# A Perceiver cross-attention's context values, computed 128 rows at a time across batches

## The chip, the cores and the metric

The kernel runs on one core of a Trainium2 chip. The metric is the device time of one execution in microseconds (us); the time before is the median of three runs. All arithmetic is in 32-bit floats. A batch norm, an exponential, a copy and the like run on VectorE (DVE), ScalarE (ACT) or GpSimd (POOL); matrix products and transposes run on TensorE (PE); SyncE's queue (SP) issues the DMAs. PEld is TensorE's loading of stationary operands, which overlaps its matmuls.

## The reference, cut to what matters

The model has two layers, each a gated cross-attention and a gated feed-forward block, on `x` (16 batches, 256 tokens, 256 features) with contexts of 77 tokens:

```python
x = x + tanh(g_xattn[0]) * L0_xattn(ctx, layernorm(x), ...)   # stage 0: Perceiver attention
x = x + tanh(g_ffn[0])   * L0_ffn(layernorm(x), ...)          # stage 1: 8 experts, the top 2 of a token
x = x + tanh(g_xattn[1]) * L1_xattn(layernorm(x), ctx, ...)   # stage 2: masked cross-attention
x = x + tanh(g_ffn[1])   * L1_ffn(layernorm(x), ...)          # stage 3: gated linear attention
```

The change lies in stage 0, whose attention is

```python
def L0_xattn(image_embeds, latents, ln1_g, ln1_b, ln2_g, ln2_b, Wq, Wkv, Wo):
    x = layer_norm(image_embeds, ln1_g, ln1_b)      # 16 x 77 x 256, the contexts
    l = layer_norm(latents, ln2_g, ln2_b)           # 16 x 256 x 256, the latents
    q = l @ Wq                                      # 256 x 1024: 16 heads of 64
    kv = concatenate([x, l], axis=1) @ Wkv          # 333 tokens x 2048
    k, v = split(kv, 2, axis=-1)
    w = softmax(q * 64 ** -0.25 @ (k * 64 ** -0.25).T)   # per batch and head, 256 x 333
    return (w @ v) @ Wo
```

Keys and values of a batch thus run over 333 tokens: 256 latents and 77 contexts.

## The kernel before

**Stages.** The four stages run one after the other. Stage 0 takes the first half of the time, then come the experts, the second attention and the gated linear attention. Routing work of stage 1 (logits, choice, scatter of rows) is done inside stage 0, batch by batch, between the attention's steps. Weights come in by DMA: those of stages 0 and 1, and `wq2`, `wk2`, `wv2`, `wo2` of the second attention (256 KB each, loaded at L133), at the start of the kernel; those of stage 3 later, into a pool that reuses stage 0's memory once that stage is over (`w3`, L778).

**A batch in stage 0.** Batch b's 77 context rows are one DMA (`load_c`, L110 to 112). Contexts and latents are normed on their own (`norm_c`, L552; `normed_all`, L565). `turn` (L571) transposes both on PE into one PSUM pair, and DVE writes them with scale and shift into `kvT`, 333 columns: latents first, then contexts. `all_values` (L586) computes the values of the 333 tokens as three chunks of `KC` = 111 rows: per chunk 2 halves of 512 columns times 2 steps over the features, so 4 matmuls; ACT copies one half of the result out of PSUM, DVE the other. `heads` (L603) computes queries and keys of two heads at a time: 2 + 2 matmuls into one PSUM pair, then ACT scales the queries and DVE copies the keys, both into the tile `qk`.

**A unit.** The attention runs over 64 units (b, g), g being a group of four heads, that is two head pairs n = 0 and 1, each with three chunks of keys c. `scores` (L617) has six steps u = 3n + c of two matmuls each; these fill three PSUM pairs, two steps to a pair, and ACT takes the exponential of each pair. POOL adds the chunks for the softmax's denominators (`sums`, L632). `values` (L641) multiplies by the values of the batch and divides; `project` (L672) applies the output weights once per batch.

**The order.** It is written out by hand in the loop over units (L711 to 751), and the engines' instructions keep it (`Pinned`, L50, so nearly all instructions of stage 0 carry line 50 in the profile; those of stage 3 carry line 1548). On PE a unit is: its scores; then the values of the unit before; in group 1 the turn of the next batch and the projection of the batch before; in group 2 the next batch's `all_values`; then `heads` of the next unit, first n = 0, then n = 1, and straight after them that unit's scores:

```python
now = scores(b, g)
...
now = sums(*now)
if behind is not None:
    values(*behind)
if g == 1 and b + 1 < B:
    turn(b + 1)
if g == 1 and b > 0:
    project(b - 1)
...
if g == 2 and b + 1 < B:
    all_values(b + 1, *route.weighted(b - 2))
if ahead is not None:
    heads(*ahead, 0)
    heads(*ahead, 1)
```

At the start two short bursts of matmuls (`warm`) are issued before the first batch. SP's DMAs go out in one order too: among them the 16 clears of 640 KB in the first two batches, the experts' inputs (`fetch`, L1074, `xin`) and the experts' row stores (L1099), and masks and contexts of the second attention (L1018 to 1024).

Of the kernel before, what the change touches and what calls it, by code (L numbers as in the profile page):

```python
# [73 lines left out]
def layers(ctx: ExitStack, tc: tile.TileContext, t, out, check):  # L74
# [30 lines left out]
    w12 = s12.enter_context(tc.tile_pool(name="s12w", bufs=1, side="right"))  # L105
    ws1 = s1.enter_context(tc.tile_pool(name="s1w", bufs=1, side="right"))
    if fast:
        ctxs = s0.enter_context(tc.tile_pool(name="f0c", bufs=3))

    def load_c(b):  # L110
        cs[b] = ctxs.tile([S2, D], F32, tag="c", name="c")
        nc.sync.dma_start(out=cs[b], in_=t["ctx"][b])

    load_x(0)
    if fast:
# [14 lines left out]
    ew1 = load_w("ew1", D, 2048, ws1)  # L130
    prio = const("prio", [P, 8])
    nc.sync.dma_start(out=prio, in_=t["prio"])
    wq2, wk2, wv2, wo2 = (load_w(n, D, D, w12) for n in ("wq2", "wk2", "wv2", "wo2"))  # L133
    if fast:
        both, own, pmask = (w12.tile(shape, F32, tag=n, name=n) for n, shape in (
            ("both", [P, 2, D]), ("own", [P, 2, 32]), ("pmask", [P, 2])))
# [233 lines left out]
    class Route:  # L370
# [162 lines left out]
    def stage0_fast():  # L533
        with ExitStack() as sx:
# [5 lines left out]
            def pair(name):  # L540
                return pairs.tile([P, 2, 512], F32, tag="ps", name=name)
# [3 lines left out]

            esum, rsum = check["esum"], check["rsum0"]

            xn, cn, kvT, v, oT = {}, {}, {}, {}, {}

            y, mvs, tallies = {}, {}, []  # L550

            def norm_c(b):  # L552
                mvs[b, "c"] = moments(cs[b].unsqueeze(1), S2, 1)

            def norm_x(b):
                mvs[b, "x"] = moments(xs[b])
# [7 lines left out]

            def normed_all(b):  # L565
                xn[b] = w1.tile([P, 2, D], F32, tag="xn", name="xn")
                cn[b] = w1.tile([S2, 1, D], F32, tag="cn", name="cn")
                normed(xn[b], y.pop(b), *mvs.pop((b, "y")))
                normed(cn[b], cs[b].unsqueeze(1), *mvs.pop((b, "c")), S2, 1)

            def turn(b):  # L571
                kvT[b] = w2.tile([P, 2, NK], F32, tag="kvT", name="kvT")
                both = pair("tr")
                for k in range(2):
                    ps = both[:, k, :]
                    for i in range(2):
                        pe.transpose(ps[:, i * P:(i + 1) * P], xn[b][:, i, k * P:(k + 1) * P], ident)
                    pe.transpose(ps[:, S:NK], cn[b][:, 0, k * P:(k + 1) * P], ident[:S2, :S2])
                for k in range(2):
                    ps = both[:, k, :]  # L580
                    dve.tensor_scalar(kvT[b][:, k, :S], ps[:, :S], vec[:, V_LN2G + k:V_LN2G + k + 1],
                                            vec[:, V_LN2B + k:V_LN2B + k + 1], ALU.mult, ALU.add)
                    dve.tensor_scalar(kvT[b][:, k, S:], ps[:, S:NK], vec[:, V_LN1G + k:V_LN1G + k + 1],
                                            vec[:, V_LN1B + k:V_LN1B + k + 1], ALU.mult, ALU.add)

            def all_values(b, *between):  # L586
                v[b] = w2.tile([KC, 3, 1024], F32, tag="v", name="v")
                for c in range(3):
                    both = pair("v")
                    for h in range(2):  # L590
                        ps = both[:, h, :]
                        for k in range(2):
                            pe.matmul(ps[:KC, :], kvT[b][:, k, c * KC:(c + 1) * KC],
                                             wkv0[:, k, 1024 + h * 512:1024 + (h + 1) * 512],
                                             start=k == 0, stop=k == 1)
                    act.copy(v[b][:, c, :512], both[:KC, 0, :])
                    dve.tensor_copy(v[b][:, c, 512:], both[:KC, 1, :])
                    for x in between[c:c + 1]:
                        x()

            qk = {}

# [14 lines left out]
            def scores(b, g):  # L617

                x_qk = qk.pop((b, g))
                e = w2.tile([KC, 6, 2, S], F32, tag="e", name="e")  # L620
                for u in range(0, 6, 2):
                    sc = pair("sc").rearrange("p j (x s) -> p j x s", x=2)
                    for x in range(2):
                        n, c = divmod(u + x, 3)
                        for j in range(2):
                            r = slice(64 * j, 64 * j + 64)
                            pe.matmul(sc[:KC, j, x, :], x_qk[r, n, S + c * KC:S + (c + 1) * KC],
                                             x_qk[r, n, :S], start=True, stop=True)
                    act.activation(e[:, u:u + 2], sc[:KC].rearrange("p j x s -> p x j s"), AF.Exp)
                return b, g, e  # L630

            def sums(b, g, e):  # L632
                es = w2.tile([KC, 2, 2 * S], F32, tag="es", name="es")
                by_chunk = e.rearrange("p (n c) j s -> p n c (j s)", n=2)
                pool.tensor_tensor(es, by_chunk[:, :, 0], by_chunk[:, :, 1], ALU.add)
                pool.tensor_tensor(es, es, by_chunk[:, :, 2], ALU.add)
                for n in range(2):
                    pool.tensor_tensor(esum[:KC], esum[:KC], es[:, n, :], ALU.add)
                return b, g, e, es

            def values(b, g, e, es, last=False):  # L641

                if g == 0:
                    oT[b] = w1.tile([P, 8, S], F32, tag="oT", name="oT")
                both = pair("o")
                den, ps = both[:, 0, :], both[:, 1, :]
                heads = [(h, slice(32 * h, 32 * h + 32)) for h in range(4)]

                for c in range(3 if last else 1):
                    for h, r in heads:  # L650
                        n, j = divmod(h, 2)
                        x = e[:, 3 * n + c, j, :] if last else es[:, n, j * S:(j + 1) * S]
                        pe.matmul(den[r, :S], ones[:KC, :32], x, start=c == 0, stop=not last or c == 2)
                for i in range(2):
                    for c in range(3):
                        for h, r in heads:
                            n, j = divmod(h, 2)
                            lo = (4 * g + h) * 64 + 32 * i
                            pe.matmul(ps[r, i * S:(i + 1) * S], v[b][:, c, lo:lo + 32], e[:, 3 * n + c, j, :],
                                      start=c == 0, stop=c == 2)  # L660
                rd = w2.tile([P, S], F32, tag="rd", name="rd")
                dve.reciprocal(rd, den[:, :S])
                dve.tensor_tensor(oT[b][:, 2 * g:2 * g + 2, :], ps.rearrange("p (i s) -> p i s", i=2),
                                  bc(rd, [P, 2, S], 1), ALU.mult)
                tallies.append((rd, rsum[:, 4 * b + g:4 * b + g + 1]))
# [110 lines left out]


    w3 = ctx.enter_context(tc.tile_pool(name="s3w", bufs=1, reuse_waits="tile"))  # L778

    def c3(name, shape):  # L780
        return w3.tile(list(shape), F32, tag=name, name=name)
# [1314 lines left out]
```

## Time and profile before

| quantity | value |
|---|---|
| median of three runs | 1918.44 us (1918.27 to 1920.98) |
| profiled execution | 1920.95 us |
| span of that execution's trace | 1919.2 us |
| mean granted TensorE clock | 0.995 of full speed |
| PE busy | 1889.1 us, 98% |
| DVE, ACT, POOL busy | 1097.6, 869.8, 992.1 us (57%, 45%, 52%) |
| matmul records | 14028 |
| DMA moved | 75.17 MB, mean 39 GB/s |

The profile is one execution. Its span reaches from the first to the last instruction; the execution's time has 1.75 us around that. A group's row gives busy time and the mean time of one instruction; matmuls are pipelined and overlap in their records, so a matmul's mean is longer than its share of the path. A 32-bit matmul leaves two records. In a row's shapes the stationary operand comes first (`128*111` is 128 partitions by 111 columns), then the moving one. "Idle before" names what the engine waited for. The clock is the one that the throttle granted to TensorE, 1.00 being full speed.

### The profile page before, as it was taken

To read this page: it belongs to the slowest core of one execution; us is meant where nothing else is said; L and a number is where in the kernel's file an instruction comes from. 1 tells how busy PE (TensorE), PEld (TensorE's weight loads), DVE (VectorE), ACT (ScalarE), POOL (GpSimd) and SP (SyncE) were. 2 spreads that over 40 slices of the span, in tenths; PEclk is the share of its full clock that TensorE was granted. 3 is DMA by queue.
4 is the path that set the end of the run, shared out by engine and by line. 5 is a ranking of instruction groups with operands and counts; after the bars stand their busy time and mean duration, and the time that the engine had idled before them with its cause. 6 is when DMAs were issued, how large, how long until landed. Compare 5 with 4: busy or idle time off the path is not lost.

```text
span 1919.2 us, 34996 instructions
## 1 busy us (share of the span) xinstructions
PE 1889.1 (98%) x14028; PEld 1314.7 (69%) x14028; DVE 1097.6 (57%) x2667; ACT 869.8 (45%) x1788; POOL 992.1 (52%) x895
## 2 busy tenths in 40 slices
PE   8999999999999999999999899999999999999997
PEld 5666666666666666666787766667777777777775
DVE  3334555455554555545464388876666666666664
ACT  3333435343353433434343478744444445454442
POOL 4644756557565575655734756314444444444433
PEclk9999999999999999999999999999999999999999
DMA  9300000000000000000068923000000000000000
GB/s 341 138 1 3 14 11 14 7 11 14 11 14 7 11 14 9 12 7 9 12 218 253 225 43 49 15 1 6 7 6 7 6 12 6 7 6 7 12 7 14
DMA packets 54108, 75.17 MB, mean 39 GB/s; under 512 B 10112, under 2 KB 43760, under 8 KB 53424
## 3 DMA queue, kind: packets, MB, share of 16 engines
q1 hardware_dynamic: 41648, 56.05, 8.7%
q0 software_dynamic: 12288, 16.79, 4.3%
q8 instruction: 113, 1.85, 0.4%
q14 instruction: 59, 0.48, 0.1%
HBM read 39.27 MB, written 33.55 MB: 38 GB/s over the span
## 4 chain that ended last, share of the span: by engine, by line
PE 95%; DVE 2%; ACT 1%; POOL 0%; DMA 0%; issue 0%; SPq 0%; DVEq 0%; ACTq 0%; POOLq 0%
PE o L50 13%; PE qk L50 13%; PE sc L50 10%; PE v L50 9%; PE proj L50 7%; PE kq L1548 6%; PE sc L1548 5%; PE ex L50 3%; PE gq L1548 3%; PE v L1548 3%; PE proj L1548 3%; PE o L1548 3%; PE gz L1548 2%; PE den L1548 2%; PE ms L1548 1%; PE low L1548 1%
## 5 line engine op out<-in xcount | busy, mean ns | idle before, releaser
L50 POOL TENSOR_SCALAR rs<-mv 128x2 f32<-128x2 f32 (+1 forms) x92 | 17.6, 191 | 456.9 <-DVE mv L50 431.1
L50 ACT ACTIVATE qk<-qk 128x256 f32<-128x256 f32 x128 | 49.3, 385 | 343.6 <-PE qk L50 343.5
L50 ACT ACTIVATE e<-sc 111x1024 f32<-111x1024 f32 x192 | 182.2, 1021 | 16.9 <-PE sc L50 16.9
L50 PE MATMUL sc<-qk 64*111 64x256 f32 x1536 | 182.2, 383 | 0.0
L50 PE MATMUL o<-e,v 111*32 111x256 f32 x3072 | 177.5, 379 | 0.0
L50 DVE RECIPROCAL rd<-o 128x256 f32<-128x256 f32 x64 | 112.3, 1755 | 101.8 <-PE o L50 101.8
L50 PE MATMUL v<-wkv,kvT 128*111 128x512 f32 x384 | 169.3, 597 | 0.6 <-DVE kvT L50 0.6
L50 PEld LDWEIGHTS sc<-qk 64*111 64x111 f32 x1536 | 132.1, 172 | 52.9 <-issue 29.0
L50 POOL TENSOR_TENSOR esum<-esum,es 111x512 f32<-111x512 f32 x128 | 163.0, 1274 | 10.0
L50 PE MATMUL qk<-kvT,wkv 128*128 128x333 f32 x512 | 164.3, 443 | 0.0
L50 POOL TENSOR_TENSOR es<-e 111x1024 f32<-111x1024 f32 x64 | 151.3, 2363 | 23.9 <-ACT e L50 22.6
L50 POOL TENSOR_TENSOR es<-es,e 111x1024 f32<-111x1024 f32 x64 | 150.4, 2349 | 5.0
L50 POOL TENSOR_TENSOR k<-e,ee 128x256 f32<-128x256 f32 x64 | 46.7, 730 | 192.2 <-ACT e L50 192.1
L50 PEld LDWEIGHTS o<-e,v 111*32 111x32 f32 x3072 | 99.8, 110 | 65.9
L50 DVE COPY qk<-qk 128x333 f32<-128x333 f32 x128 | 64.6, 504 | 124.0 <-ACT qk L50 122.6
L50 PE MATMUL qk<-kvT,wq 128*128 128x256 f32 x512 | 134.3, 385 | 0.0
L50 PEld LDWEIGHTS v<-wkv,kvT 128*111 128x111 f32 x384 | 67.0, 177 | 91.7 <-issue 90.2
L50 POOL TENSOR_TENSOR at<-at,at 128x768 f32<-128x768 f32 x63 | 113.9, 1807 | 24.3 <-DVE at L50 24.3
L50 DVE TENSOR_TENSOR at<-sc,amask 128x768 f32<-128x768 f32 x64 | 61.3, 958 | 113.7 <-PE sc L1548 110.1
L50 POOL DMA_INDIRECT x<-rows_out,pos x64 | 99.9, 1561 | 34.6 <-issue 15.4
L50 PEld LDWEIGHTS qk<-kvT,wkv 128*128 128x128 f32 x512 | 97.2, 190 | 30.0
L50 PEld LDWEIGHTS qk<-kvT,wq 128*128 128x128 f32 x512 | 94.3, 189 | 34.0 <-issue 13.2
(250 smaller groups left out, 4141.2 us busy)
## 6 DMA issues: line engine op xcount, KB each, us to landing
rows<-zero SPq DMA_DIRECT2D x16, 640.0 KB
xin<-rows SPq DMA_DIRECT2D x16, 640.0 KB
rows_out<-y SPq DMA_DIRECT2D x16, 384.0 KB
x<-in_x_dram SPq DMA_DIRECT2D x16, 256.0 KB
rows_out<-y SPq DMA_DIRECT2D x16, 256.0 KB
out_dram<-x SPq DMA_DIRECT2D x15, 256.0 KB
wkv<-in_wkv_dram SPq DMA_DIRECT2D x2, 1024.0 KB
ew<-in_ew_dram SPq DMA_DIRECT2D x2, 1024.0 KB
```

The source lines that it names most:

```text
L50: x = getattr(self.engine, name)(*a, **k)
L1548: tc.keep_in_program_order(nc.tensor.matmul(*a, **k))
```

## The change

Five things change, all in the fast path.

1. *Contexts by 128 rows.* The 16 × 77 = 1232 context rows are taken as 10 chunks of up to 128 rows, across batches. A chunk is loaded, normed, transposed and turned into values with the batch in which it begins (`c_new`: batches 0, 1, 3, 4, 6, 8, 9, 11, 13 and 14). Its pool `f0c` has two buffers, not three.
2. *Context keys.* A chunk's transposed rows lie in `ctxT`; ACT copies the pieces that belong to batch b into `kvT[b]`, one or two pieces per batch.
3. *Context values by DRAM.* A chunk's values go from PSUM to `vc`, from there by DMA to a DRAM tile per batch (`vctx`), and from there by DMA into chunk 2 of `v[b]`. Batch 0 takes its own straight from PSUM.
4. *Chunks of a batch.* The three chunks of 111 rows become two of 128 latents and one of 77 contexts, in scores, sums and values. `all_values` has two chunks of matmuls for a batch, and a third where a context chunk begins. The six steps of `scores` fill the PSUM pairs as (0, 1), (3, 4), (2, 5), no longer as (0, 1), (2, 3), (4, 5), so that the steps of a pair have the same number of rows.
5. *Weights of the second attention.* `wq2`, `wk2`, `wv2`, `wo2` are loaded after stage 0 into the pool `w3`, no longer at the start.

The core of the diff:

```diff
-        ctxs = s0.enter_context(tc.tile_pool(name="f0c", bufs=3))
+        ctxs = s0.enter_context(tc.tile_pool(name="f0c", bufs=2))
+    c_rows = B * S2
+    c_new = {b: j for j in range(-(-c_rows // P)) for b in [P * j // S2]}
...
     def load_c(b):
-        cs[b] = ctxs.tile([S2, D], F32, tag="c", name="c")
-        nc.sync.dma_start(out=cs[b], in_=t["ctx"][b])
+        if b in c_new:
+            j, n = c_new[b], c_count(c_new[b])
+            cs[b] = ctxs.tile([P, D], F32, tag="c", name="c")
+            nc.sync.dma_start(out=cs[b][:n], in_=t["ctx"].rearrange("b s d -> (b s) d")[P * j:P * j + n])
...
-    wq2, wk2, wv2, wo2 = (load_w(n, D, D, w12) for n in ("wq2", "wk2", "wv2", "wo2"))
+    if not fast:
+        wq2, wk2, wv2, wo2 = (load_w(n, D, D, w12) for n in ("wq2", "wk2", "wv2", "wo2"))
...
+            chunks = [slice(0, P), slice(P, S), slice(S, NK)]
+            counts = [P, P, S2]
...
             def turn(b):
...
-                    pe.transpose(ps[:, S:NK], cn[b][:, 0, k * P:(k + 1) * P], ident[:S2, :S2])
+                    if n:
+                        pe.transpose(ps[:, S:S + n], cn[b][:n, 0, k * P:(k + 1) * P], ident[:n, :n])
+                if n:
+                    ctxT[j] = w2.tile([P, 2, P], F32, tag="ctxT", name="ctxT")
...
+                for j, at, to, n in c_pieces(b):
+                    act.copy(kvT[b][:, :, S + to:S + to + n], ctxT[j][:, :, at:at + n])
...
             def all_values(b, *between):
-                v[b] = w2.tile([KC, 3, 1024], F32, tag="v", name="v")
-                for c in range(3):
-                    both = pair("v")
-                    for h in range(2):
-                        ps = both[:, h, :]
-                        for k in range(2):
-                            pe.matmul(ps[:KC, :], kvT[b][:, k, c * KC:(c + 1) * KC],
-                                             wkv0[:, k, 1024 + h * 512:1024 + (h + 1) * 512],
-                                             start=k == 0, stop=k == 1)
-                    act.copy(v[b][:, c, :512], both[:KC, 0, :])
-                    dve.tensor_copy(v[b][:, c, 512:], both[:KC, 1, :])
...
+                v[b] = w2.tile([P, 3, 1024], F32, tag="v", name="v")
+                if b in c_new:
+                    j = c_new[b]
+                    n = c_count(j)
+                    both = some_values(ctxT[j][:, :, :n], n)
+                    vc = w1.tile([P, 1024], F32, tag="vc", name="vc")
+                    copied(vc, both, n)
+                    if b == 0:
+                        copied(v[b][:, 2, :], both, S2)
+                    for to in range(1, B):
+                        for jj, at, row, n in c_pieces(to):
+                            if jj == j:
+                                nc.sync.dma_start(out=vctx[to][row:row + n], in_=vc[at:at + n, :])
+                if b > 0:
+                    nc.sync.dma_start(out=v[b][:S2, 2, :], in_=vctx[b])
+                for c in range(2):
+                    copied(v[b][:, c, :], some_values(kvT[b][:, :, chunks[c]], P), P)
...
             def scores(b, g):
...
-                for u in range(0, 6, 2):
+                for slot in ((0, 1), (3, 4), (2, 5)):
                     sc = pair("sc").rearrange("p j (x s) -> p j x s", x=2)
-                    for x in range(2):
-                        n, c = divmod(u + x, 3)
+                    rows = counts[slot[0] % 3]
+                    for x, u in enumerate(slot):
+                        n, c = divmod(u, 3)
                         for j in range(2):
                             r = slice(64 * j, 64 * j + 64)
-                            pe.matmul(sc[:KC, j, x, :], x_qk[r, n, S + c * KC:S + (c + 1) * KC],
+                            pe.matmul(sc[:rows, j, x, :], x_qk[r, n, S + chunks[c].start:S + chunks[c].stop],
                                              x_qk[r, n, :S], start=True, stop=True)
-                    act.activation(e[:, u:u + 2], sc[:KC].rearrange("p j x s -> p x j s"), AF.Exp)
+                    act.activation(e[:rows, slot[0]:slot[1] + 1:slot[1] - slot[0]],
+                                   sc[:rows].rearrange("p j x s -> p x j s"), AF.Exp)
...
     w3 = ctx.enter_context(tc.tile_pool(name="s3w", bufs=1, reuse_waits="tile"))
+    if fast:
+        wq2, wk2, wv2, wo2 = (load_w(n, D, D, w3) for n in ("wq2", "wk2", "wv2", "wo2"))
```

`some_values` holds the four matmuls of a chunk of values, `copied` its two copies out of PSUM (ACT 512 columns, DVE 512); `c_pieces(b)` lists which rows of which chunks are batch b's.

More of the change, by code (lines that the diff above doesn't have):

```diff
@@ L107, in layers, with c_count, c_pieces @@
     if fast:
-        ctxs = s0.enter_context(tc.tile_pool(name="f0c", bufs=3))
+        ctxs = s0.enter_context(tc.tile_pool(name="f0c", bufs=2))
+    c_rows = B * S2
+    c_new = {b: j for j in range(-(-c_rows // P)) for b in [P * j // S2]}
+    def c_count(j):
+        return min(P, c_rows - P * j)
+    def c_pieces(b):
+        lo, hi = b * S2, (b + 1) * S2
+        return [(j, max(lo, P * j) - P * j, max(lo, P * j) - lo, min(hi, P * j + P) - max(lo, P * j))
+                for j in range(lo // P, (hi - 1) // P + 1)]
     def load_c(b):
-        cs[b] = ctxs.tile([S2, D], F32, tag="c", name="c")
-        nc.sync.dma_start(out=cs[b], in_=t["ctx"][b])
+        if b in c_new:
+            j, n = c_new[b], c_count(c_new[b])
+            cs[b] = ctxs.tile([P, D], F32, tag="c", name="c")
+            nc.sync.dma_start(out=cs[b][:n], in_=t["ctx"].rearrange("b s d -> (b s) d")[P * j:P * j + n])
     load_x(0)
@@ L546, in stage0_fast @@
             esum, rsum = check["esum"], check["rsum0"]
-            xn, cn, kvT, v, oT = {}, {}, {}, {}, {}
+            xn, cn, kvT, v, oT, ctxT = {}, {}, {}, {}, {}, {}
+            vctx = [tc.dram_tile([S2, 1024], F32, name=f"vctx{b}") for b in range(B)]
+            chunks = [slice(0, P), slice(P, S), slice(S, NK)]
+            counts = [P, P, S2]
             y, mvs, tallies = {}, {}, []
             def norm_c(b):
-                mvs[b, "c"] = moments(cs[b].unsqueeze(1), S2, 1)
+                if b in c_new:
+                    n = c_count(c_new[b])
+                    mvs[b, "c"] = moments(cs[b][:n].unsqueeze(1), n, 1)
             def norm_x(b):
@@ L566, in normed_all @@
                 xn[b] = w1.tile([P, 2, D], F32, tag="xn", name="xn")
-                cn[b] = w1.tile([S2, 1, D], F32, tag="cn", name="cn")
                 normed(xn[b], y.pop(b), *mvs.pop((b, "y")))
-                normed(cn[b], cs[b].unsqueeze(1), *mvs.pop((b, "c")), S2, 1)
+                if b in c_new:
+                    n = c_count(c_new[b])
+                    cn[b] = w1.tile([P, 1, D], F32, tag="cn", name="cn")
+                    normed(cn[b][:n], cs[b][:n].unsqueeze(1), *mvs.pop((b, "c")), n, 1)
             def turn(b):
@@ L573, in turn @@
                 both = pair("tr")
+                j = c_new.get(b)
+                n = 0 if j is None else c_count(j)
                 for k in range(2):
@@ L582, in turn @@
                                             vec[:, V_LN2B + k:V_LN2B + k + 1], ALU.mult, ALU.add)
-                    dve.tensor_scalar(kvT[b][:, k, S:], ps[:, S:NK], vec[:, V_LN1G + k:V_LN1G + k + 1],
-                                            vec[:, V_LN1B + k:V_LN1B + k + 1], ALU.mult, ALU.add)
-            def all_values(b, *between):
-                v[b] = w2.tile([KC, 3, 1024], F32, tag="v", name="v")
-                for c in range(3):
-                    both = pair("v")
-                    for h in range(2):
-                        ps = both[:, h, :]
-                        for k in range(2):
-                            pe.matmul(ps[:KC, :], kvT[b][:, k, c * KC:(c + 1) * KC],
-                                             wkv0[:, k, 1024 + h * 512:1024 + (h + 1) * 512],
-                                             start=k == 0, stop=k == 1)
-                    act.copy(v[b][:, c, :512], both[:KC, 0, :])
-                    dve.tensor_copy(v[b][:, c, 512:], both[:KC, 1, :])
-                    for x in between[c:c + 1]:
-                        x()
+                    if n:
+                        dve.tensor_scalar(ctxT[j][:, k, :n], ps[:, S:S + n], vec[:, V_LN1G + k:V_LN1G + k + 1],
+                                                vec[:, V_LN1B + k:V_LN1B + k + 1], ALU.mult, ALU.add)
@@ new lines, in turn, with some_values, copied @@
+                for j, at, to, n in c_pieces(b):
+                    act.copy(kvT[b][:, :, S + to:S + to + n], ctxT[j][:, :, at:at + n])
+            def some_values(x, n):
+                both = pair("v")
+                for h in range(2):
+                    for k in range(2):
+                        pe.matmul(both[:n, h, :], x[:, k, :], wkv0[:, k, 1024 + h * 512:1024 + (h + 1) * 512],
+                                         start=k == 0, stop=k == 1)
+                return both
+            def copied(to, both, n):
+                act.copy(to[:n, :512], both[:n, 0, :])
+                dve.tensor_copy(to[:n, 512:], both[:n, 1, :])
@@ new lines, in all_values @@
+            def all_values(b, *between):
+                v[b] = w2.tile([P, 3, 1024], F32, tag="v", name="v")
+                between = list(between)
+                if b in c_new:
+                    j = c_new[b]
[13 more added lines that the diff above has]
+                    copied(v[b][:, c, :], some_values(kvT[b][:, :, chunks[c]], P), P)
+                    if between:
+                        between.pop(0)()
+                for x in between:
+                    x()
@@ L619, in scores @@
                 x_qk = qk.pop((b, g))
-                e = w2.tile([KC, 6, 2, S], F32, tag="e", name="e")
-                for u in range(0, 6, 2):
+                e = w2.tile([P, 6, 2, S], F32, tag="e", name="e")
+                for slot in ((0, 1), (3, 4), (2, 5)):
                     sc = pair("sc").rearrange("p j (x s) -> p j x s", x=2)
-                    for x in range(2):
-                        n, c = divmod(u + x, 3)
+                    rows = counts[slot[0] % 3]
+                    for x, u in enumerate(slot):
+                        n, c = divmod(u, 3)
                         for j in range(2):
                             r = slice(64 * j, 64 * j + 64)
-                            pe.matmul(sc[:KC, j, x, :], x_qk[r, n, S + c * KC:S + (c + 1) * KC],
+                            pe.matmul(sc[:rows, j, x, :], x_qk[r, n, S + chunks[c].start:S + chunks[c].stop],
                                              x_qk[r, n, :S], start=True, stop=True)
-                    act.activation(e[:, u:u + 2], sc[:KC].rearrange("p j x s -> p x j s"), AF.Exp)
+                    act.activation(e[:rows, slot[0]:slot[1] + 1:slot[1] - slot[0]],
+                                   sc[:rows].rearrange("p j x s -> p x j s"), AF.Exp)
                 return b, g, e
             def sums(b, g, e):
-                es = w2.tile([KC, 2, 2 * S], F32, tag="es", name="es")
+                es = w2.tile([P, 2, 2 * S], F32, tag="es", name="es")
                 by_chunk = e.rearrange("p (n c) j s -> p n c (j s)", n=2)
                 pool.tensor_tensor(es, by_chunk[:, :, 0], by_chunk[:, :, 1], ALU.add)
-                pool.tensor_tensor(es, es, by_chunk[:, :, 2], ALU.add)
+                pool.tensor_tensor(es[:S2], es[:S2], by_chunk[:S2, :, 2], ALU.add)
                 for n in range(2):
-                    pool.tensor_tensor(esum[:KC], esum[:KC], es[:, n, :], ALU.add)
+                    pool.tensor_tensor(esum, esum, es[:, n, :], ALU.add)
                 return b, g, e, es
@@ L651, in values @@
                         n, j = divmod(h, 2)
-                        x = e[:, 3 * n + c, j, :] if last else es[:, n, j * S:(j + 1) * S]
-                        pe.matmul(den[r, :S], ones[:KC, :32], x, start=c == 0, stop=not last or c == 2)
+                        rows = counts[c]
+                        x = e[:rows, 3 * n + c, j, :] if last else es[:, n, j * S:(j + 1) * S]
+                        pe.matmul(den[r, :S], ones[:rows, :32], x, start=c == 0, stop=not last or c == 2)
                 for i in range(2):
@@ L658, in values @@
                             lo = (4 * g + h) * 64 + 32 * i
-                            pe.matmul(ps[r, i * S:(i + 1) * S], v[b][:, c, lo:lo + 32], e[:, 3 * n + c, j, :],
+                            rows = counts[c]
+                            pe.matmul(ps[r, i * S:(i + 1) * S], v[b][:rows, c, lo:lo + 32], e[:rows, 3 * n + c, j, :],
                                       start=c == 0, stop=c == 2)
```

## Prediction

> **What bounds the kernel now.** I read the page first: its busy times, its slices, and the shares of the chain that ended last.
>
> ```profile
> PE 1889.1 (98%) x14028; PEld 1314.7 (69%) x14028; DVE 1097.6 (57%) x2667; ACT 869.8 (45%) x1788; POOL 992.1 (52%) x895
> PE   8999999999999999999999899999999999999997
> PE 95%; DVE 2%; ACT 1%; POOL 0%; DMA 0%; issue 0%; SPq 0%; DVEq 0%; ACTq 0%; POOLq 0%
> ```
>
> PE is the bound: 98% of the span and 95% of the chain. Next the windows, by stage (us, PE, weight loads, DVE, ACT, POOL, clock, DMA share, GB/s):
>
> ```profile
> 60.00:64.00 4.00, 4.00 (x13) 2.08 (x12) 0.81 (x2) 1.00 (x2) 0.00 (x0) 1.00 1.09 385
> 200.00:300.00 100.00, 100.00 (x794) 66.60 (x794) 53.42 (x127) 41.38 (x79) 65.88 (x50) 1.00 0.04 12
> 1016.00:1020.00 4.00, 4.00 (x25) 3.57 (x24) 3.07 (x11) 1.26 (x3) 1.53 (x2) 1.00 0.39 132
> ```
>
> In stage 0 PE has no gap and DMA is nearly idle, except while rows are cleared (60 to 64 us). So any PE time taken out is gained, and any wait put in is lost. PE's waits from 20 to 960 us are only these (total, times, longest):
>
> ```profile
> PE o L50 <- POOL es L50: 1.8, 1, 1.8
> PE rtr L50 <- ACT rxn L50: 1.2, 2, 1.1
> ```
>
> The groups by shape (busy, mean ns) give the work that changes; the chain gives one batch's values:
>
> ```profile
> L50 PE MATMUL sc<-qk 64*111 64x256 f32 x1536 | 182.2, 383 | 0.0
> L50 PE MATMUL v<-wkv,kvT 128*111 128x512 f32 x384 | 169.3, 597 | 0.6 <-DVE kvT L50 0.6
> L50 PE MATMUL tr<-ident,cn 77*128 77x77 f32 x32 | 7.6, 238 | 0.0
> 234.67 10.30 PE v L50 x24
> ```
>
> Last, the timeline where one unit (batch, four heads) ends its projections and starts its scores, with the fifth and seventh pair of weight loads:
>
> ```profile
> 957.08 2.43 PEld L50 LDWEIGHTS sc<-qk 64*111 64x111 f32 x24 [0.46 <-issue]
> 957.08 2.85 PE L50 MATMUL sc<-qk 64*111 64x256 f32 x24
> 957.18 0.39 ACT L50 ACTIVATE qk<-qk 128x256 f32<-128x256 f32 x1 [1.54 <-PE qk L50]
> 957.60 0.50 DVE L50 COPY qk<-qk 128x333 f32<-128x333 f32 x1 [1.42 <-ACT qk L50]
> 957.82 0.18 PEld L50 LDWEIGHTS sc<-qk 64*111 64x111 f32 x2
> 958.25 0.18 PEld L50 LDWEIGHTS sc<-qk 64*111 64x111 f32 x2
> ```
>
> Scores run in 12 passes (2 records of 64 rows side by side), 0.215 us each (958.25 − 957.82 over two). The copy of the second head pair's keys ends at 958.10, while scores of the first pair already run. The seventh pass, the first that needs these keys, loads at 958.25: it is covered by 0.15 us.
>
> **The change part by part.** *Values.* A batch's values are 3 blocks of 4 matmuls, 10.30/3 = 3.43 us each. The matmul's cost goes by its 512 moving columns, so 128 rows should cost what 111 did. Before: 16 × 3 = 48 blocks. After: 16 × 2 for latents and 10 for contexts, 42. Six fewer, all on PE without a gap: **−20.6 us**.
>
> *Order of the scores.* Pairs of units (0,1), (2,3), (4,5) become (0,1), (3,4), (2,5). Unit 3 is the first of the second head pair; it moves from the seventh pass to the fifth. Its weights would load at 957.82, 0.28 us before the copy ends, and the copy cannot come earlier: it follows ACT's scaling of the queries, which follows the last key matmul, as in the rows above; I found the same offsets in all 64 units. So a new wait of PE for DVE arises. From an operand's end to the weight load, the nearest row is a wait of an expert for its transpose:
>
> ```profile
> 1068.07 0.56 ACT L50 COPY xT<-xT 128x512 f32<-128x512 f32 x1
> 1068.68 0.30 PEld L50 LDWEIGHTS ex<-ew,xT 128*128 128x128 f32 x2 [0.94 <-ACT xT L50]
> ```
>
> 1068.68 − 1068.63 = 0.05 us. Then one load that no matmul hides: 2.43/24 = 0.10 us for 111 columns, 0.11 for 128. The copy ends 1.03 us after the unit's first load (mean of the units), so the fifth pass starts at 1.03 + 0.05 + 0.11 = 1.19 us. Unstalled, in the old sizes, it starts at 0.09 + 4 × 0.215 = 0.95. Loss 0.24 us a unit (0.237 unrounded), which also holds the 0.01 us that 128 columns add to the unit's first load. **64 × 0.237 = +15.2 us.** Bounds: without the latency and with a faster load 0.21 (13.3 us); with 0.06 us more latency 0.30 (19.2 us). Nothing downstream gives it back, as PE is the bound.
>
> *Transposes of contexts.* 32 of 77 columns become 20 of 128: 32 × 77 = 2,464 columns against 2,560, so about 0 (in the trace each starts 0.07 us after the one before: 2.2 us on the path, whatever the 7.6 us busy).
>
> *Start.* The first context load has 128 rows, and the first values wait for one more DVE step of the contexts: taken as +0.5 us, between 0 and 1. The two waits shown above shrink, because PE arrives there 0.24 us later while POOL and ACT do not: −0.5 us together (0 to −1.2; POOL's own order fixes their ends).
>
> *ACT and DVE.* ACT gets 25 copies of context keys into the transposed tile (about 0.37 us each, as ACT's copies of 256 columns), in the unit where the next batch is turned, ahead of its query scaling. There I trace the second copy's wait for DVE through the queue: the first head pair's scaling moves from 465.5 to 466.1 us, its key copy ends at 467.0, and the scores need it at 467.27. Cover 0.27 us; if it is gone, at most 0.3 us in some 10 units, 3 us. Value copies are 42 pairs instead of 48; POOL's sums keep their free sizes, so both are 0.
>
> *Contexts' values through DRAM.* 24 writes and 15 reads of 77 × 4 KB join SP's queue; each write waits for the DVE copy of its block. Behind them on SP are only context loads a batch ahead. The read of batch b is needed at its first values, over 34 us after its issue; a 256 KB load of x took 2.9 us after its issue. Batch 1's is queued behind the clearing of rows (DMA full until about 65 us), lands near 75 us and is needed near 90. Cost 0; without the cover, the whole lateness falls on the batch's first values.
>
> *Second attention's weights.* 4 × 256 KB move from the start to the seam of stages 0 and 1, ahead on SP of the experts' row stores, mask loads and the fourth expert's input. That input's issue moves from 979.6 to about 982.4 us; it is needed near 993. The 1 MB is about 3 us at 340 GB/s, and the window at 1016 shows slack. Bound 0 to +4 us, taken +0.5.
>
> Sum: −20.6 + 15.2 + 0.5 − 0.5 + 0.5 = **−4.9 us**. The profiled execution took 1920.95 us (span 1919.2) and would take 1916.0; it lies 2.5 us above the median of 1918.44. On the median: **1913.5 us**. About 0.2% (3.8 us) is what measurement can tell: faster is below 1914.6, slower above 1922.3.
>
> **A rule beside the rows.** The wait of 1.06 us at 172 us was followed by 3.4 us of granted clock 0.5, the wait of 1.80 us at 38 us was not:
>
> ```profile
> 172.02 0.33 PE L50 MATMUL rtr<-ident,rxn 128*128 128x128 f32 x1 [1.06 <-ACT rxn L50]
> 172.51 0.55 PE L50 MATMUL rtr<-ident,rxn 128*128 128x128 f32 x3 [0.16 <-ACT rxn L50]
> 172.89 4.43 PE L50 MATMUL v<-wkv,kvT 128*111 128x512 f32 x6
> ```
>
> That stretch cost 1.7 us (12.00 us for its values, not 10.30). By rows, gaps of 0.24 us each 10 us or more should not set it off. The Trainium skill, page "TensorE: Matmul & The Clock Gate", section "HAM oscillation — how this bites in real kernels", speaks against the change: waits between bursts can throttle the clock each time anew. By that, 64 waits × 1.7 us would add 109 us; I leave it out.
>
> **The rivals.** (1) *The reorder is free*: the keys' copy is early enough, or PE runs ahead by another way. The sum without 15.2 us is −20.1: about 1898. Against: the 0.28 us above. (2) *Slower, by a longer wait*: each pass five waits s; the change loses once 64 s > 19.7 + 0.4, s > 0.31 us. At s = 0.40 (latency 0.16 us more than the one row, or ACT late by its new copies, which now counts at once since the 0.15 us cover is gone) it is +5.5: about 1924. Against: the latency row and the constant offsets. (3) *Seam and cover*: the weights' 1 MB (up to 4) or ACT's copies (up to 3) cost their upper bounds: 1917 to 1920. (4) *It doesn't do what it says*: a batch's contexts return from DRAM late; 1 us in each of 15 batches gives 1928. Against: 34 us of cover.
>
> **How the numbers follow.** Forecast 0.58 (own range 1909.5 to 1918, from the stall's bounds 13.3 to 19.2 with the small terms); rival 1 0.06, rival 2 0.15, rival 3 0.17, rival 4 0.04. Range 1909 to 1921: forecast, rival 3 and the near part of rival 2; left out are rivals 1 and 4 and most of 2, about 0.2. Faster: 0.42 of the forecast's 0.58 and rival 1: 0.48. Same: 0.16 of the forecast, rival 3 and 0.01 of rival 2: 0.34. Slower: the rest, 0.18.
>
> **What the changed profile would show.** The value matmuls 336 records, near 148 us. A new line in PE's waits, scores for DVE's copy, near 64 × 0.24 us, and in the timeline the fifth pair of loads right after that copy. No wait of the outputs' matmuls for a DMA, none of an expert for its input. Without the scores' wait, rival 1 is right; with 0.3 us or more each, rival 2; granted clock of 0.5 within stage 0 would mean the rule. A wait of weights or experts near 980 to 1020 us is rival 3.

## The result, and the profile after

The changed kernel took 1920.43 us (median of 12 runs, 1912.89 to 1926.33), the kernel before 1920.3 us (12 runs, 1918.23 to 1922.1) on the same chip: ratio 1.0004, 95% interval 0.9993 to 1.0015. Nothing was gained; forecast were 1913.5 us and a gain of 4.9. The spread of the changed kernel goes with the mean clock granted to TensorE in each run: 1912.89 us came with 0.997, 1926.33 us with 0.990, and a line through all 12 runs gives 1.7 us for each 0.001 of clock. The page's first lines, as shown of the kernel before:

```profile
PE 1890.7 (98%) x13968; PEld 1309.8 (68%) x13968; DVE 1057.8 (55%) x2632; ACT 871.8 (45%) x1802; POOL 987.7 (51%) x883
PE   8999999999999999999998999999999999999997
PE 94%; DVE 2%; DMA 2%; ACT 1%; SPq 1%; POOL 0%; issue 0%; POOLq 0%; DVEq 0%; ACTq 0%
```

PE is still the bound, but DMA and SP's queue have come into the chain with 3% where they had 0%. The groups by shape, and two batches' values in the chain:

```profile
L50 PE MATMUL sc<-qk 64*128 64x256 f32 x1024 | 141.8, 402 | 0.5 <-DVE qk L50 0.5
L50 PE MATMUL sc<-qk 64*77 64x256 f32 x512 | 65.9, 376 | 0.0
L50 PE MATMUL v<-wkv,kvT 128*128 128x512 f32 x256 | 112.5, 592 | 0.0
L50 PE MATMUL v<-wkv,ctxT 128*128 128x512 f32 x72 | 34.3, 621 | 1.0 <-DVE ctxT L50 1.0
...
235.17 10.30 PE v L50 x24
295.88 6.87 PE v L50 x16
```

A block of values still takes 3.43 us (10.30 for three, 6.87 for two): the six blocks are gone as counted. The wait for the keys' copy is there too, but not where the forecast said that it would show. PE's waits from 20 to 960 us, then those of its weight loads (the first lines of each):

```profile
PE o L50 <- POOL es L50: 1.5, 1, 1.5
PE rtr L50 <- ACT rxn L50: 1.0, 2, 0.8
PE sc L50 <- DVE qk L50: 0.5, 1, 0.5
```

```profile
PEld v L50 <- issue: 71.0, 295, 0.4
PEld sc L50 <- issue: 27.6, 60, 0.5
PEld sc L50 <- DVE qk L50: 24.5, 67, 1.0
```

In the profile a matmul's end is modelled, and it covers a wait of 0.22 us; the weight loads tell it: 24.5 us of idleness before them, where the kernel before has 0.5, and of which a part is the ordinary pause between loads. The timeline of the unit that starts at 951.35 us shows one:

```profile
951.35 0.73 PEld L50 LDWEIGHTS sc<-qk 64*128 64x128 f32 x8 [0.46 <-issue]
951.88 0.50 DVE L50 COPY qk<-qk 128x333 f32<-128x333 f32 x1 [1.42 <-ACT qk L50]
952.44 1.55 PEld L50 LDWEIGHTS sc<-qk 64*128 64x128 f32 x16 [0.35 <-DVE qk L50]
```

Eight loads are four passes; the fifth pair waits for the copy's end at 952.38 and loads 0.06 us later. Stage 0 ends with its last projection, and the second attention begins with the keys of its contexts. Before, then after:

```profile
968.02 7.26 PE L50 MATMUL proj<-wo0h,oT 128*128 128x256 f32 x32
...
1022.25 2.24 PE L50 MATMUL k<-cT,wk 128*128 128x308 f32 x8
```

```profile
964.82 5.00 PE L50 MATMUL proj<-wo0h,oT 128*128 128x256 f32 x22
...
1024.41 2.24 PE L50 MATMUL k<-cT,wk 128*128 128x308 f32 x8
```

Stage 0 took 969.8 us, 975.3 before: 5.5 us less. What came after took it back. PE's waits from 960 to 1030 us, before and after:

```profile
PE ex L50 <- ACT xT L50: 0.3, 1, 0.3
```

```profile
PE xT L50 <- DMA xin<-rows: 4.5, 1, 4.5
PE xT L50 <- DVE x L50: 0.4, 1, 0.4
```

The transposes of expert 7 (the eighth) wait 4.5 us for their input. Its issue and its first use in the timelines, before and then after:

```profile
1006.89 0.34 SPq L1074 DMA_DIRECT2D xin<-rows  x1
...
1015.97 0.60 PE L50 MATMUL xT<-ident,xin 128*128 128x128 f32 x4
```

```profile
1008.97 0.34 SPq L1136 DMA_DIRECT2D xin<-rows  x1
...
1015.36 1.09 PE L50 MATMUL xT<-ident,xin 128*128 128x128 f32 x4 [4.54 <-DMA xin<-rows]
```

Counted from the end of stage 0, the issue was at 31.6 us and is now at 39.2; the input was needed at 40.7 before, and now takes 6.4 from its issue until the transposes start. After the wait PE also runs at half clock for a while (windows; clock, DMA share and GB/s last):

```profile
1010.00:1015.00 5.00, 0.82 (x4) 0.38 (x2) 2.18 (x9) 0.00 (x0) 0.96 (x1) 0.91 0.86 275
1015.00:1020.00 5.00, 4.64 (x15) 4.02 (x16) 1.26 (x5) 1.17 (x2) 0.96 (x1) 0.50 0.47 178
```

From the end of stage 0 to the second attention's contexts, the kernel before took 46.97 us, the changed one 54.60: of the 7.6 us, 4.5 are the wait and 2.8 the slower clock (from expert 7's first transpose to the contexts 9.05 us, for 6.28).

### The profile page after: what moved, and what is told of

The parts are those of the page before. It is cut to its first block, busy times and chain, and to the rows that moved or that the text cites. A ratio compares the mean times of both kernels' runs of the same rounds, so it can differ in the third digit from the quotient of the medians.

```text
span 1924.5 us, 34997 instructions
## 1 busy us (share of the span) xinstructions
PE 1890.7 (98%) x13968; PEld 1309.8 (68%) x13968; DVE 1057.8 (55%) x2632; ACT 871.8 (45%) x1802; POOL 987.7 (51%) x883
## 4 chain that ended last, share of the span: by engine, by line
PE 94%; DVE 2%; DMA 2%; ACT 1%; SPq 1%; POOL 0%; issue 0%; POOLq 0%; DVEq 0%; ACTq 0%
PE o L50 13%; PE qk L50 13%; PE sc L50 11%; PE v L50 8%; PE proj L50 7%; PE kq L1610 6%; PE sc L1610 5%; PE ex L50 3%; PE gq L1610 3%; PE v L1610 3%; PE proj L1610 3%; PE o L1610 3%; PE gz L1610 2%; PE den L1610 2%; PE low L1610 2%; PE q L50 1%
## 5 line engine op out<-in xcount | busy, mean ns | idle before, releaser
L50 PE MATMUL sc<-qk 64*128 64x256 f32 (+1 forms) x1536 | 197.1, 393 | 0.5 <-DVE qk L50 0.5
L50 ACT ACTIVATE e<-sc 128x1024 f32<-128x1024 f32 (+1 forms) x192 | 186.9, 1017 | 18.7 <-PE sc L50 17.7
L50 PE MATMUL o<-e,v 128*32 128x256 f32 (+1 forms) x3072 | 177.9, 379 | 0.0
L50 PEld LDWEIGHTS sc<-qk 64*128 64x128 f32 (+1 forms) x1536 | 126.6, 172 | 71.9 <-issue 27.6
L50 POOL TENSOR_TENSOR esum<-esum,es 128x512 f32<-128x512 f32 x128 | 162.2, 1267 | 10.0
L50 POOL TENSOR_TENSOR es<-e 128x1024 f32<-128x1024 f32 x64 | 151.8, 2372 | 17.4 <-ACT e L50 16.0
L50 POOL TENSOR_TENSOR es<-es,e 77x1024 f32<-77x1024 f32 x64 | 150.3, 2349 | 5.0
L50 PEld LDWEIGHTS o<-e,v 128*32 128x32 f32 (+1 forms) x3072 | 99.9, 110 | 66.3
L50 PE MATMUL proj<-wo0h,oT 128*128 128x256 f32 x512 | 113.5, 380 | 0.0
L50 PE MATMUL v<-wkv,kvT 128*128 128x512 f32 x256 | 112.5, 592 | 0.0
```

What stands on the lines that cost most here:

```text
L50: x = getattr(self.engine, name)(*a, **k)
```

## The experiments

**First set: which part costs what.** Two edits, alone and together, and the weights' part by itself.

*The order of the score pairs alone.*

```diff
-                for slot in ((0, 1), (3, 4), (2, 5)):
+                for slot in ((0, 1), (2, 5), (3, 4)):
```

> The change with one edit: the pairs of score steps are (0,1), (2,5), (3,4), so that the second head pair's keys are first needed in the seventh pass again. Theory: each of 64 units loses 0.22 us in the changed kernel to the wait for the keys' copy, 14 us in all, and the seam of stages 0 and 1 loses another 5 us at the median to a late expert input. Then this kernel takes 1906 us, PE's fifth pass starts 0.86 us after the first in each unit, and the expert's wait stays as it is. Rival: PE's time in stage 0 is not what the end hangs on (the experts wait for rows from DRAM anyway): 1918 to 1921 us, with a longer wait of the experts in place of the 14 us.

Measured: 1902.99 us (6 runs), ratio 0.9909 (0.9891 to 0.9927). The time hangs on stage 0, and the stall was real: a unit's scores, from the start of the first matmul to the start of the last, are 2.49 us where the changed kernel has 2.70. The fifth pass starts 0.97 us after the first, not 0.86 as expected. The time is 3 us less than expected, with the expert's wait still there (4.3 us); this goes with the granted clock, whose mean over the runs is 0.9948 here and 0.9928 in the changed kernel, 3.4 us at 1.7 us for each 0.001.

*The late weights alone, in the kernel before.*

```diff
-    wq2, wk2, wv2, wo2 = (load_w(n, D, D, w12) for n in ("wq2", "wk2", "wv2", "wo2"))
+    if not fast:
+        wq2, wk2, wv2, wo2 = (load_w(n, D, D, w12) for n in ("wq2", "wk2", "wv2", "wo2"))
...
+    if fast:
+        wq2, wk2, wv2, wo2 = (load_w(n, D, D, w3) for n in ("wq2", "wk2", "wv2", "wo2"))
```

> The kernel before with part 5 of the change alone (the second attention's four weights loaded after stage 0). Theory: these loads make the experts' inputs late, whatever stage 0 does: 1922 to 1926 us, with a wait of an expert's transpose for its input, and the runs spread over some 10 us. Rival: the loads cost nothing, and the inputs are late in the changed kernel for another reason: 1918 to 1921 us and no such wait.

Measured: 1929.05 us (6 runs, 1923.71 to 1931.91), ratio 1.005 (1.0034 to 1.0065). Part 5 of the change alone loses 8.5 us by the medians (1920.52 for the kernel before on this chip), more than expected, and the same input is waited for (its PE waits, 960 to 1030 us, the first lines). Not all of it is waiting: the mean granted clock is 0.9922, against 0.9947 in those runs of the kernel before.

```profile
PE xT L50 <- DMA xin<-rows: 4.6, 1, 4.6
PE ex L50 <- ACT xT L50: 2.0, 2, 1.7
```

*The weights in stage 0's last batch, in memory that is free by then.*

```diff
-                y[b] = w1.tile([P, 2, D], F32, tag="y", name="y")
+                y[b] = wl.tile([P, 2, D], F32, tag="y", name="y")    # xn and vc likewise; wl stays open
...
+                if (b, g) == (B - 1, 0):
+                    wvo = wl.tile([P, 2, 2, D], F32, tag="vc", name="wvo")
+                    late.extend((wl.tile([P, 2, D], F32, tag="y", name="wq2"),
+                                 wl.tile([P, 2, D], F32, tag="xn", name="wk2"), wvo[:, 0], wvo[:, 1]))
+                    for w, x in zip(late, ("wq2", "wk2", "wv2", "wo2")):
+                        nc.sync.dma_start(out=w, in_=t[x].rearrange("(k p) f -> p k f", p=P))
...
-        wq2, wk2, wv2, wo2 = (load_w(n, D, D, w3) for n in ("wq2", "wk2", "wv2", "wo2"))
+        wq2, wk2, wv2, wo2 = late
```

> The changed kernel, but the second attention's weights are loaded in the last batch of stage 0, into the memory of the tiles y, xn and vc, which are free from then on (these three tiles lie in a pool of their own that stays open). Theory: no load at the seam, so no wait for an expert's input: 1914 us, which is the forecast, with runs within 4 us of each other. Rival: the loss is not the weights': 1918 to 1921 us, spread as before.

Measured: 1912.52 us (12 runs), ratio 0.9961 (0.9948 to 0.9973). The wait is gone, and from the end of stage 0 to the contexts it takes 46.9 us again. The spread, 1909.23 to 1919.83, is wider than expected; the two runs above 1914 us have a granted clock of 0.992, the others 0.995 to 0.997.

*Both edits.*

> Both edits together: pairs of score steps (0,1), (2,5), (3,4), and the weights loaded in the last batch of stage 0. Theory: 20.6 us of values gained, nothing lost to the keys' copy or at the seam: 1899 to 1901 us. Rival (stage 0 is not what the end hangs on): not under 1912 us.

Measured: 1898.44 us (5 runs, 1895.57 to 1902.5), ratio 0.9881 (0.9864 to 0.9899), the fastest of all: this is the version to keep. Against the one before it the order of the pairs is worth 14.1 us (1912.52 − 1898.44), as counted from 64 × 0.22 = 14.1.

**Second set: bytes or order.** The loss at the seam, the passage from stage 0 to stage 1, comes with the late weights. But is it their 1 MB on the DMA engines, or their place in SP's queue? In stage 1 the order of SP's DMAs is made by the scheduler, and adding four loads made it another one: experts' inputs 3 to 7 went out after 1, 3, 5, 6, 8 row stores before, and after 1, 4, 6, 8, 10 in the changed kernel. Behind a store, an input waits for that store's expert.

*The weights on ACT's queue.*

```diff
-        wq2, wk2, wv2, wo2 = (load_w(n, D, D, w3) for n in ("wq2", "wk2", "wv2", "wo2"))
+        wq2, wk2, wv2, wo2 = (w3.tile([P, 2, D], F32, tag=n, name=n) for n in ("wq2", "wk2", "wv2", "wo2"))
+        for w, n in ((wq2, "wq2"), (wk2, "wk2"), (wv2, "wv2"), (wo2, "wo2")):
+            nc.scalar.dma_start(out=w, in_=t[n].rearrange("(k p) f -> p k f", p=P))
```

> The changed kernel, but the second attention's weights are issued by ACT's DMA queue, not SP's; on SP the experts' inputs then stand nearly as early among the row stores as in the kernel before. The bytes at the seam are the same. Theory (SP's order makes the inputs late): 1912 to 1915 us. Rival (the extra 1 MB makes them late, whichever queue): 1919 to 1922 us, with a wait of 2 us or more for an expert's input.

Measured: 1920.96 us (12 runs), ratio 1.0 (0.999 to 1.0009). By the total the rival is right, by the trace it is not: no expert waits for an input (expert 7's is issued 28.9 us after stage 0, and the contexts start after 47.5 us), with the same bytes at the seam (issued from 968.5 us on; stage 0 ends at 969.7). The time goes to a new wait, among the contexts; the trace is of the slowest of the 12 runs, 1927.46 us. SP's waits from 1005 to 1025 us, PE's from 940 to 1150, and SP's timeline:

```profile
SPq L1138 <- DMA rows<-xw,pos: 10.4, 1, 10.4
```

```profile
PE k L50 <- DVE vc L50: 4.8, 1, 4.8
```

```profile
1020.77 0.35 SPq L1138 DMA_DIRECT2D xin<-rows  x1
1021.22 0.31 SPq L1084 DMA_DIRECT2D mk<-in_maskT_dram  x1
```

In this order the last mask stands behind an input that SP holds for 10.4 us, until the last rows are scattered. DVE waits for the mask, and PE for the DVE steps behind it.

*An order fixed by hand, with and without the load.* All of stage 1's DMAs on SP are issued in the order of the code (`sp = Pinned(tc, nc.sync)`): with the inputs late and no load at the seam; with the inputs early (`fetch(x + 3)` behind the transposes of expert x) and the load behind the first three inputs; and with the load ahead of these.

> No load at the seam (the weights come in the last batch of stage 0), but SP's order there is fixed by hand so that each expert's input stands as late among the row stores as in the changed kernel: inputs 3 to 7 after 2, 4, 6, 8, 10 stores; in the changed kernel after 1, 4, 6, 8, 10, in the kernel before after 1, 3, 5, 6, 8. Theory (order): the late inputs come back without any extra byte, 1917 to 1921 us and a wait for an input. Rival (bytes): 1912 to 1914 us, no such wait.

> The changed kernel with its 1 MB of weights at the seam, right behind the first three inputs, but SP's order behind them fixed by hand with the experts' inputs early: inputs 3 to 7 after 1, 3, 5, 7, 9 stores. Theory (order): 1912 to 1915 us, no wait for an input. Rival (bytes): 1918 to 1922 us with a wait for an input, as the 1 MB is 3 us of full DMA.

> As the kernel with the inputs' order fixed early, but the weights stand on SP ahead of the first input, so that they wait only for the last projection that reads the old weights, near 949 us, and move while DMA is idle. By either theory: 1911 to 1914 us, no wait for an input; a wait here would mean that fixing the order by hand costs something itself.

Measured: 1927.71 us, ratio 1.004 (1.0027 to 1.0054); 1919.86 us, 1.0004 (0.9994 to 1.0014); 1921.05 us, 1.0006 (0.9997 to 1.0015). The first says that an order can cost 15 us against the same kernel without it (1912.52; by the ratios too), with no byte at the seam; it waits four times for an input, 10.5 us in all, and some 4 of the 15 us go with its granted clock (0.9930, for 0.9953). The other two, which both wait three times for an input (3.8 and 5.2 us in all), say that with this order it is all the same whether the 1 MB moves at the seam or 14 us earlier (issued at 951 us, not 965). But the three missed what they were to compare: the code's order puts mask loads ahead, and SP stands until a mask buffer is free. SP's waits from 960 to 1010 us of the first, two of its lines (the kernel before has 9.7 us in ten waits for `uneven`, at most 2.4 each):

```profile
SPq L50 <- DVE uneven L50: 20.0, 8, 5.3
SPq L50 <- DVE y L50: 9.8, 2, 7.1
```

So the expectation for the second and third failed on a fault of the experiment, and two more were made with the exact orders.

*The exact order of before with the load, and the exact order of after without it.* Each DMA of stage 1 on SP is put down as a function and called when the written-out order comes to it (x input, m mask, c contexts, s store, w weights):

```diff
+            line = list("xxxwwwwmcmcmcsxcccssxcscccsmxmsccmxsmcmsccmsmxmmsmsmcmssmxsxsxs")   # with the load
+            line = list("xxxsmcmcmcxssccscxmsccmscxmsmccmscmxmmsmccmsmcmxsmcsssxsxsx")       # without it
+            def put(kind, issue):
+                held[kind].append(issue)
+                while line and held[line[0]]:
+                    held[line.pop(0)].pop(0)()
...
```

> The changed kernel with its 1 MB of weights at the seam, but SP's order there written out by hand exactly as in the kernel before, the four weights put in behind the first three inputs. The kernels with a hand-made order so far also moved the mask loads ahead, which hold SP until a mask buffer is free; this one doesn't. Theory (the order that the scheduler made around the new loads costs the time, not their bytes): 1912 to 1915 us, expert 7's input issued about 32 us after the end of stage 0, no wait for it. Rival (the bytes): 1918 to 1922 us and a wait for an input of 3 us or more.

> No load at the seam (weights in the last batch of stage 0), but SP's order there written out by hand exactly as in the changed kernel, without the four weights. Theory (order): 1917 to 1921 us, expert 7's input issued 37 us or more after the end of stage 0 and waited for. Rival (bytes): 1912 to 1914 us and no wait.

Measured: 1914.62 us (7 runs), ratio 0.9961 (0.9947 to 0.9974), no wait for an input; and 1917.23 us (12 runs), ratio 0.9977 (0.9968 to 0.9986), with this wait (960 to 1030 us):

```profile
PE xT L50 <- DMA xin<-rows: 4.1, 1, 4.1
PE xT L50 <- DVE x L50: 0.4, 1, 0.4
```

Expert 7's input on SP, in the one and in the other (stage 0 ends at 967.62 and 967.52 us):

```profile
999.11 0.34 SPq L50 DMA_DIRECT2D xin<-rows  x1
```

```profile
1005.86 0.34 SPq L50 DMA_DIRECT2D xin<-rows  x1
```

Ratios to the kernel before, with stage 0 as in the changed kernel:

| SP's order at the seam | no load there | 1 MB there |
|---|---|---|
| that of before | 0.9961 | 0.9961 |
| that of after | 0.9977 | 1.0004 |

In the order of before the 1 MB costs nothing. In the order of after the inputs are late even without it, which costs 3 us (0.0016 × 1920; 2.6 by the medians of the last two kernels, which ran on one chip). Expert 7's input went out 31.5, 31.5, 38.3 and 39.2 us after stage 0, reading the table by rows, against a need at 40.7. So the theory of the order holds.

The corner below right is 5 us above its neighbour, but that these are the price of the bytes is not shown. From the end of stage 0 to the contexts the traces, by rows, take 46.89, 46.86, 54.06 and 54.60 us: at the seam the 1 MB costs 0.5 us where the inputs are late. Most of the rest goes with the clock, whose mean over the runs is, in the same order, 0.9953, 0.9947, 0.9950 and 0.9928: at 1.7 us for each 0.001, the last step of 0.0022 is 3.7 us.

Nor is all that is lost at the seam lost in the end: 7.2 us there (54.06 − 46.86) are 3 in the whole. A later wait of PE, for the second attention's tile `pg`, is 1.8 us shorter in the exact order of after than in that of before (that of before first, 940 to 1110 us):

```profile
PE o L50 <- DVE pg L50: 3.1, 1, 3.1
```

```profile
PE o L50 <- DVE pg L50: 1.3, 2, 0.9
```

The slower clock behind it takes less too: 0.93 in the window from 1050 to 1100 us in the first, about 3.5 us, and 0.98 in that from 1100 to 1200 us in the second, about 2.

## Why the prediction was wrong

*Values, −20.6 us: right.* Blocks of 3.43 us, 42 of them.

*Order of the scores, +15.2 us: right.* The fifth pair of loads stands 1.08 us after the unit's first, as worked out (1.03 + 0.05), and a unit's scores, from the first matmul's start to the last one's, take 2.703 us where the old sizes and order have 2.472 (means of the 64 units): 0.231 us, 14.8 in all, for 0.237 and 15.2. Undoing it returned 14.1 us; with the new sizes in the old order a unit takes 2.487 us, so 0.015 us a unit, 1 us in all, stay.

*Start, transposes, ACT's copies, the round trip through DRAM: right in that none shows on the path.* In stage 0 no line of PE's waits names them, apart from the start: the first values wait 1.0 us for the contexts' DVE step and begin at 13.4 us, 12.8 before, 0.6 later for 0.5 taken. The two old waits shrink from 3.0 to 2.5 us, as taken. Stage 0 as a whole: forecast −5.4 us (−20.6 + 15.2 + 0.5 − 0.5), found −5.5 (975.3 to 969.8). Both executions have a stretch of 3.4 us at half clock in it, the kernel before in its third batch's values, the changed one at the start (0.57 in the window from 14 to 18 us), so that the two cancel.

*Second attention's weights, taken +0.5 us, bound +4: this is the step that failed.* It cost 8 us (0.0043 × 1920): some 3 by late inputs, net of what comes back behind the seam, 0.5 by the bytes, and some 4 with the granted clock of the runs. The prediction followed one input, the fourth, and found its issue moved by 2.8 us to 982.4, with the need near 993. That was right (it was 3.3 us later, and nobody waited), but the shift grows down the queue, to 7.5 us at expert 7, whose issue had 9.1 us in hand before, and the input takes 6.4. The four loads were counted at the first place in SP's queue only; the order that the scheduler made behind it was not looked at. The third rival had the place, at 1917 to 1920, and nearly the size. Its bound of 4 us came from the 1 MB's transfer time, which is the wrong quantity: with the order of before the transfer is free.

*With the seam mended* the ratio is 0.9961, a gain of 7.5 us. In the trace of the kernel with the weights in stage 0, that stage ends at 967.65 us, 7.6 earlier than in the kernel before, whose stretch at half clock (1.7 us) it doesn't have; 5.9 remain, against 5.4 forecast.

*A part is open.* Why the granted clock is lower in the runs of the changed kernel (0.9928) and of the late weights alone (0.9922) than in all the others but one (0.9930, with the late inputs of the order made by hand) isn't known; the kernel before has 0.9944 to 0.9952 on three chips, and the kernel with the pairs in the old order alone has the same load, the same order on SP and the same late input, and 0.9948. Nor does the changed kernel's profiled execution (1926.33 us, the slowest of its 12 runs) stand for its median; the verdict on the seam rests on the runs.

*The rule that was weighed.* The wait of 4.5 us was followed by a stretch at half clock; 64 waits of 0.22 us were not: the granted clock from 200 to 900 us is 1.00 in every window (the stretch from 14 to 18 us lies ahead of the first of these waits), and the 109 us that the prediction left out did not come. The Trainium skill, page "TensorE: Matmul & The Clock Gate", section "HAM oscillation — how this bites in real kernels", sums its rule up as no PE idle gaps over some 3.4 us. By this bound it never spoke against waits of 0.24 us; the prediction took the rule without it. These two rows agree with the bound, but others don't: besides the wait of 1.06 us at 172 us in the kernel before, the waits for `pg`, of 3.1 us before and 1.2 us after, are followed by a slower clock too (each with the window behind it, the clock third from the end):

```profile
1100.46 0.63 PE L50 MATMUL o<-pg,vd 77*32 77x256 f32 x4 [3.12 <-DVE pg L50]
1100.00:1105.00 5.00, 4.12 (x32) 1.54 (x32) 3.80 (x4) 2.76 (x4) 1.01 (x1) 0.64 0.39 66
```

```profile
1100.75 0.63 PE L50 MATMUL o<-pg,vd 77*32 77x256 f32 x4 [1.24 <-DVE pg L50]
1101.00:1106.00 5.00, 4.59 (x48) 1.93 (x44) 3.67 (x5) 2.94 (x7) 1.02 (x1) 0.69 0.38 54
```

## What to carry to other kernels

When a change moves a DMA, read the whole order of that queue in both programs, down to the last transfer that somebody waits for, and set each one's issue plus its time to land against its need: a shift that is harmless at the head can grow behind it. Ask of a reordering of matmuls which operand is first used earlier, and when that operand is ready: a cover of 0.15 us, lost 64 times, ate some seven tenths of what the values gained, and keeping both (pairs in the old order of need, loads in idle time) gave 22 us. Where kernels differ by a few microseconds, set the granted clocks of their runs side by side before putting the difference down to the code. An experiment that pins an order must pin the exact one, or it tests something else.

## What the runs showed of the hardware that was not expected

A wait of PE of 0.22 us doesn't show in PE's own row of waits (0.5 us in all, for 14), since the matmuls' ends are modelled; the row of the weight loads shows it (24.5 us). The cost of a wait for data can be more than the wait: after 4.5 us without work PE ran at a granted clock of 0.50 in the window from 1015 to 1020 us, which made 4.5 us into 7.3 at that place, though a part came back at a later wait. And the changed kernel's runs differ by 0.7% (1912.89 to 1926.33 us), most of which goes with their granted clock (0.997 to 0.990).
